# Self-attention's output projection by seven block products, and two weight loads of the first cross-attention query issued earlier

## The chip, the cores and the metric

The kernel runs on one core of one Trainium2 chip. A core has five engines that run side by side: TensorE (PE in the profile; PEld is its weight load), VectorE (DVE), ScalarE (ACT), GpSimd (POOL) and SyncE (SP), which here only issues DMA transfers. The metric is the device time of one execution in microseconds (us); less is better. Everything is in float32.

## What is computed

One decoder layer on x, 8 batches of 256 tokens with 1024 features: causal self-attention, layer norm, cross-attention to a context, layer norm, and a feed-forward part with a memory. The change touches the last product of the self-attention. In the reference that is:

```
out = jnp.einsum('bhqk,bhkd->bhqd', attn, v)
out = out.transpose(0, 2, 1, 3).reshape(bsz, q_len, HIDDEN)
return out @ wo.T
...
x = _layernorm(x + _L0_attn_ref(x, L0_attn_wq, L0_attn_wk, L0_attn_wv, L0_attn_wo), axis=-1)
```

For each batch this is a product of the heads' outputs (256 tokens x 1024) with a 1024 x 1024 matrix, added to x. The change's second part touches the query projection of the cross-attention, `q = query @ Wq`.

## The kernel before, in words

`self_attention` runs 64 steps, s = 8b + c: batch b (0 to 7), chunk c (0 to 7) of 128 features, that is four heads of 32. Even and odd steps differ: a step with odd s multiplies the weights of two chunks with the values (`weighted`, L322, in two parts) and writes the two chunks' outputs, transposed, into one tile `oT` (L347, six buffers). A step also computes scores and softmax of the next chunk (`scores`, L264), the query projection of the chunk after next (`query`, L259), one item of `others` (L406), and up to four "products" of the cross-attention's keys and values, which are computed ahead in the steps 4 to 59 (L497, L525). The last steps, 62 and 63, take the first products of the cross-attention's queries in their place.

`project_out(b, i)` (L367) is the output projection. It is an item of `others` in the steps c = 0 to 3 of the following batch, b + 1: item i computes 128 tokens x 512 columns with eight matmuls of 128x512 (two instructions each, since a float32 matmul shows as two) into one PSUM bank, and VectorE adds the bank to x, which lies in `res` (L378). Behind i = 2 and 3 it also takes the layer norm's moments (L380); GpSimd computes the reciprocal root (L132), and the normalisation itself (L383) comes in the next step. The steps c = 5 and 6 transpose the result and store it (`turn`, L389).

Its weights come through `load_out` (L359): a half of the matrix, four transfers of 512 KB, into the tile `sa_wo` with four buffers. Half 0 is issued at the end of step c = 6, half 1 at the end of step c = 1 (L571, L581).

Three engines run in the order in which the program is written: PE, POOL and SP (`manual_schedule`, L98). SP's transfers are one queue: a transfer whose buffer isn't free yet holds all behind it. Most weights pass through `weights` (L105), which hands out one of nine buffers (`w4`, W4 = 9) and issues the load at once. The order on VectorE and ScalarE is set by a planner at build time, from modelled costs.

The cross-attention's projections are already done by a seven-product scheme (`seven`, L736): for a matrix cut in 2 x 2 blocks, seven block products and some additions replace eight block products. Its weight sums are formed by GpSimd during the self-attention and stored in DRAM: `sum_event` (L489) issues the loads of one sum and finishes the one before it (four additions or subtractions, L423, and the stores). `steps` (L485, L486) says in which step which event falls: 16 events for keys and values in the steps 1 to 14, the rest from step 15 on. In `seven`, each product that needs a new weight loads it when it is called (p1, p6, p5, p4; L773, L784, L790, L807); with `eager` only p1's weight is loaded ahead (L743). `eager` is used once, for the first query: `xa_early` (L615), called at the end of step 61, calls `xa_query(0, eager=True)` and then issues the loads of x1 (the self-attention's result, transposed, L642), of the rope tables (L664) and of the first keys (L668). Those go to memory that the self-attention's own buffers held until then.

Of the kernel before, what the change touches and what calls it, by code (L numbers as in the profile page):

```python
# [71 lines left out]
class Layer:  # L72
# [74 lines left out]
    def self_attention(self):  # L147
# [78 lines left out]
            nc.vector.tensor_tensor(turned, turned, sin, ALU.mult)  # L226
            nc.vector.tensor_tensor(dst, turned, dst, ALU.add)

        kTs, vs, v_d, qTs, ats, oTs = {}, {}, {}, {}, {}, {}

        def keys(b, i):
            if i == 0:
# [89 lines left out]
        def weighted(s, rest):  # L322
# [29 lines left out]
                )  # L352
            for u in range(2):
                oTs[s - 1 + u] = oT[:, u, :]

        wos = {}
        norms = []

        def load_out(b, half):  # L359
            cols = slice(half * 512, (half + 1) * 512)  # L360
            wos[b, half] = []
            for c in range(0, KC, 2):
                w = sp.tile([P, 2, 512], F32, name="sa_wo", bufs=4)
                nc.sync.dma_start(out=w, in_=a["sa_wo"][:, c : c + 2, cols])
                wos[b, half].append(w)

        def project_out(b, i):  # L367
            half, tt = divmod(i, 2)
            t = 2 * b + tt
            cols = slice(half * 512, (half + 1) * 512)  # L370
            ps = self.mm()
            for c in range(KC):
                nc.tensor.matmul(  # L373
                    ps, lhsT=oTs[b * KC + c][:, tt * P : (tt + 1) * P], rhs=wos[b, half][c // 2][:, c % 2, :],
                    start=(c == 0), stop=(c == KC - 1),
                )
            x = self.res[t]
            nc.vector.tensor_tensor(x[:, cols], ps, x[:, cols], ALU.add)  # L378
            if half == 1:
                mv, rstd = self.moments(x, EPS)  # L380

                def norm():
                    nc.vector.tensor_scalar(x, x, mv[:, 0:1], rstd, ALU.subtract, ALU.mult)  # L383
                    self.x1[t] = self.dram.tile([P, E], F32, name=f"x1_{t}")
                    nc.scalar.dma_start(out=self.x1[t], in_=x)

                norms.append(norm)

        def turn(b, tt):  # L389

# [15 lines left out]
        def others(s):  # L406
# [1 line left out]

            b, c = divmod(s, KC)
            parts = []  # L410
            if b and c < 4:
                parts.append(lambda: project_out(b - 1, c))
            elif c < 4 or 1 < b + 1 < B:
                parts.append([
# [36 lines left out]
        def sums_of_outputs(g, u, half):  # L451
# [13 lines left out]
            def run():  # L465
# [6 lines left out]
                    nc.gpsimd.dma_start(out=self.wsums["xa_wo", g][i][:, u, cols], in_=t)  # L472
            return run


        sums = [lambda n=n, m=m, i=i: sums_of_inputs(n, m, i)
                for m in range(XA_KV // 2) for n in ("xa_wk", "xa_wv") for i in range(2)]
        sums += [lambda m=m, i=i: sums_of_inputs("xa_wq", m, i) for m in range(QP) for i in range(2)]
        sums += [lambda g=g, u=u, i=i: sums_of_outputs(g, u, i)
                 for g in range(XA_KV) for u in range(2) for i in range(2)]  # L480

        n = XA_KV * 2
        steps = [1 + e * 7 // 8 for e in range(n)]  # L485
        steps += [15 + e * (KV_END - 17) // (len(sums) - n) for e in range(len(sums) - n + 1)]  # L486
        made = []

# [26 lines left out]
        for s in range(last):  # L515
# [61 lines left out]
                event()  # L577
            if c == 7 and b + 1 < B:
                load_values(b + 1, 0)
            if b and c == 1:  # L580
                load_out(b - 1, 1)  # L581
            if b and c == 0 and b + 1 < B:
                load_x(b + 1)
            if first:
# [151 lines left out]
    def seven(self, name, m, xb, turned, done, eager=False):  # L736
# [4 lines left out]
        now = {}  # L741
        if eager:
            now["a"] = self.weights([P, KC, XA_D], self.a[name][2 * m])  # L743

        def product(w, block):
            ps = self.mm()
# [34 lines left out]
            add(now["c1"][:, :S], ps, now["p1"])  # L781

        def p6():
            now["s24"] = self.weights([P, KC, XA_D], self.wsums[name, m][0])  # L784
            ps = product(now["s24"][:, :4, :], "T2")
            now["u2"] = half()
            add(now["u2"], ps, now["p1"])

        def p5():
            now["s31"] = self.weights([P, KC, XA_D], self.wsums[name, m][1])  # L790
            ps = product(now["s31"][:, 4:, :], "T1")
            now["u5"] = half()
            add(now["u5"], ps, now["u2"])
# [811 lines left out]
```

## Time and profile before

| what | value |
|---|---|
| median of three runs | 3473.19 us (3465.23, 3473.19, 3473.85) |
| the profiled execution: its own time / its span | 3463.37 us / 3461.6 us |
| mean granted TensorE clock in it | 0.988 |
| busy share of the span: PE, PEld, DVE, ACT, POOL | 97%, 71%, 61%, 35%, 30% |
| the self-attention's share of the span | about the first 1240 us |
| `project_out`'s matmuls (L373) on the chain that ended last | 6% of the span |

The page gives for each engine the time in which it was busy, the chain of work that ended last (followed back from the last instruction, at each step to what released it), and groups of instructions: line, engine, operation, output<-inputs, shape, count, then busy time and mean duration of one, then the idle time just before them and what ended it. The windows view gives the busy time of every engine, the granted clock and the DMA engines' share for a stretch of time; the timeline lists instructions in order, with the idle time of their engine before them in brackets. Matmul instructions overlap, so a group's time on the path is read from the chain, not from the mean duration.

### The profile page before, as it was taken

Reading aid. Unit: us, or ns where it says so; the run is one execution under the profiler, and the core shown is the slowest. Engines: PE = TensorE matmul, PEld = TensorE weight load, DVE = VectorE, ACT = ScalarE, POOL = GpSimd, SP = SyncE. Lnnn points to the kernel's source line nnn. Section 1 sums busy time; section 2 is a strip of 40 time slices with the busy share of each in tenths; the row PEclk is TensorE's granted clock in tenths of the full one; section 3 lists DMA queues with packets and bytes.
Section 4 is the critical chain, followed back from the end, with each engine's and each line's share of the span. In section 5 each row is a group of like instructions: output and inputs, shape, how many; then the busy total and the mean of one; then the engine's idle time right before and its main releaser. Section 6 shows DMA issues by size and latency. Waiting matters only on the chain.

```text
span 3461.6 us, 71080 instructions
## 1 busy us (share of the span) xinstructions
PE 3369.3 (97%) x27811; PEld 2443.5 (71%) x27811; DVE 2109.8 (61%) x6003; ACT 1202.3 (35%) x4030; POOL 1044.9 (30%) x1363
## 2 busy tenths in 40 slices
PE   8999999999999799999999999999999999999996
PEld 6787778787777567777767667667667766766763
DVE  4655556565565455665685666675666666566556
ACT  3444334333443343333233332233333323333224
POOL 3444655666665121111221111112111212121112
PEclk9999999999999899999999999999999999999998
DMA  7777788787886464444544344444444544344442
GB/s 254 236 258 250 269 268 279 257 273 258 296 271 221 156 215 141 143 135 134 171 149 140 123 134 142 150 137 156 138 128 133 167 142 147 128 132 135 129 146 98
DMA packets 269710, 626.36 MB, mean 181 GB/s; under 512 B 28992, under 2 KB 99792, under 8 KB 268480
## 3 DMA queue, kind: packets, MB, share of 16 engines
q1 hardware_dynamic: 194832, 441.00, 38.9%
q0 software_dynamic: 50032, 154.66, 13.8%
q10 hardware_dynamic: 24512, 26.15, 2.2%
q8 instruction: 221, 3.62, 0.4%
q14 instruction: 113, 0.93, 0.1%
HBM read 526.93 MB, written 94.77 MB: 180 GB/s over the span
## 4 chain that ended last, share of the span: by engine, by line
PE 87%; DVE 6%; DMA 2%; ACT 2%; POOL 2%; issue 2%; SPq 0%; POOLq 0%; DVEq 0%; ACTq 0%
PE mm L757 26%; PE mm L963 20%; PE mm L214 7%; PE mm L910 7%; PE mm L373 6%; PE sc L859 6%; PE mm L751 5%; PE sc L339 3%; PE mm L1241 2%; PE mm L243 1%; PE sc L273 1%; PE mm L1018 1%; POOL acc L992 1%; ACT att L295 1%; DMA w<-in_sa_wq 0%
## 5 line engine op out<-in xcount | busy, mean ns | idle before, releaser
L757 PE MATMUL mm<-x1T,w 128*128 128x256 f32 x3584 | 851.9, 382 | 13.7 <-DMA w<-xa_wq_sums 10.8
L757 PEld LDWEIGHTS mm<-x1T,w 128*128 128x128 f32 x3584 | 676.9, 190 | 199.0 <-issue 94.8
L963 PE MATMUL mm<-w,xoS 128*128 128x512 f32 x992 | 449.2, 595 | 0.0
L873 ACT ACTIVATE xatt<-xatt,nmax 128x256 f32<-128x256 f32 x512 | 257.2, 503 | 508.1 <-DVE nmax L868 496.2
L676 POOL DMA_DIRECT2D v<-v x256 | 150.9, 596 | 735.1 <-PE mm L910 617.1
L963 PE MATMUL mm<-w,xoT 128*128 128x512 f32 x744 | 338.1, 596 | 5.3 <-ACT xoT L918 4.1
L963 PEld LDWEIGHTS mm<-w,xoS 128*128 128x128 f32 x992 | 184.9, 190 | 193.1 <-issue 170.9
L214 PE MATMUL mm<-xT,w 128*128 128x256 f32 x1280 | 305.0, 395 | 3.1 <-DMA xT<-in_xT 2.9
L763 DVE TENSOR_TENSOR half<-mm,half 128x256 f32<-128x256 f32 x288 | 119.7, 416 | 291.1 <-PE mm L757 273.2
L214 PEld LDWEIGHTS mm<-xT,w 128*128 128x128 f32 x1280 | 245.4, 196 | 54.8 <-issue 19.0
L910 PEld LDWEIGHTS mm<-xat,v 32*128 32x128 f32 x8192 | 244.3, 187 | 53.4 <-issue 29.3
L929 POOL TENSOR_TENSOR xoS<-xoT 128x512 f32<-128x512 f32 x62 | 79.0, 1274 | 671.8 <-ACT xoT L918 671.5
L910 PE MATMUL mm<-xat,v 32*128 32x128 f32 x8192 | 270.2, 278 | 5.4 <-DVE acc L970 4.4
L295 ACT ACTIVATE att<-att,nmax 128x128 f32<-128x128 f32 (+1 forms) x512 | 225.5, 442 | 143.0 <-DVE nmax L290 142.8
L859 PE MATMUL sc<-kT,qT 128*128 128x256 f32 x1024 | 262.7, 380 | 0.0
L879 ACT ACTIVATE xatt<-xatt,rec 128x256 f32<-128x256 f32 x512 | 231.1, 499 | 88.0 <-DVE rec L877 87.6
L918 ACT COPY xoT<-mm 128x128 f32<-128x128 f32 x512 | 98.0, 276 | 470.2 <-PE mm L910 439.2
L763 DVE TENSOR_TENSOR raw<-mm,half 128x256 f32<-128x256 f32 x384 | 159.1, 414 | 159.3 <-PE mm L757 118.3
L423 POOL TENSOR_TENSOR ws<-ws 128x256 f32<-128x256 f32 x320 | 242.1, 757 | 26.2 <-DMA ws<-in_xa_wk 5.7
L963 PEld LDWEIGHTS mm<-w,xoT 128*128 128x128 f32 x744 | 138.7, 190 | 148.1 <-issue 127.3
L893 DVE STREAM_TRANSPOSE xat<-xatt 128x512 f32<-128x512 f32 x256 | 180.8, 707 | 74.6 <-ACT xatt L879 71.9
L373 PE MATMUL mm<-sa_wo,sa_oT 128*128 128x512 f32 x512 | 224.8, 592 | 0.0
(230 smaller groups left out, 4859.9 us busy)
## 6 DMA issues: line engine op xcount, KB each, us to landing
w<-xa_wq_sums SPq DMA_DIRECT2D x128, 512.0 KB, 3.6
w<-xa_wo_sums SPq DMA_DIRECT2D x124, 512.0 KB, 3.6
w<-in_xa_wo SPq DMA_DIRECT2D x97, 512.0 KB, 4.2
w<-in_sa_wq SPq DMA_DIRECT2D x64, 512.0 KB, 9.1
sa_wo<-in_sa_wo SPq DMA_DIRECT2D x64, 512.0 KB, 7.0
w<-in_xa_wq SPq DMA_DIRECT2D x64, 512.0 KB, 3.5
v<-v POOLq DMA_DIRECT2D x256, 128.0 KB, 3.1
w<-xa_wk_sums SPq DMA_DIRECT2D x32, 512.0 KB, 8.5
```

What stands on the lines that cost most here:

```text
L214: nc.tensor.matmul(ps[:, :S], lhsT=lhs[:, k, :], rhs=xT[:, k, :], start=(k == 0), stop=(k == KC - 1),)
L295: nc.scalar.activation(att[:, jj, lo:hi], att[:, jj, lo:hi], AF.Exp, bias=nmax[:, i : i + 1], scale=-1.0, accum_out=sums[:, i : i + 1],)
L373: nc.tensor.matmul(ps, lhsT=oTs[b * KC + c][:, tt * P : (tt + 1) * P], rhs=wos[b, half][c // 2][:, c % 2, :], start=(c == 0), stop=(c == K ...
L423: nc.gpsimd.tensor_tensor(out, in0, in1, op)
L757: nc.tensor.matmul(ps[:, :S], lhsT=w[:, k, :], rhs=rhs[:, k, :], start=(k == 0), stop=(k == 3))
L763: nc.vector.tensor_tensor(out, in0, in1, ALU.add)
L859: nc.tensor.matmul(sc[:, qt, :], lhsT=qT[:, q0 : q0 + P], rhs=kT[:, b * S : (b + 1) * S], start=True, stop=True,)
L873: nc.scalar.activation(att[:, qt, :], att[:, qt, :], AF.Exp, bias=nmax[:, qt : qt + 1], scale=-1.0, accum_out=sums[:, qt : qt + 1],)
L879: nc.scalar.activation(att[:, qt, :], att[:, qt, :], AF.Identity, bias=0.0, scale=rec[:, qt : qt + 1])
L893: self.nc.vector.transpose(self.ats[M, b][:, :, u].rearrange("p c t j -> p t c j"), self.atts[H][b].rearrange("p t (c j) -> p t c j", j=32),)
L910: nc.tensor.matmul(banks[i][:, :P], lhsT=v[rows, c, :], rhs=at[rows, c, :], start=(c == 0), stop=(c == BLOCKS - 1),)
L963: nc.tensor.matmul(ps, lhsT=oT[lhs][:, u, off + p * P : off + (p + 1) * P], rhs=w[:, u, :], start=(u == 0), stop=(u == 1),)
```

## The change

For the batches b = 1 to 6 the four items of `project_out` are replaced by `out_by_seven(b, c)`. The heads' outputs are cut into blocks A11, A12 (tokens 0 to 127; features 0 to 511 and 512 to 1023), A21, A22 (tokens 128 to 255), the matrix into B11 to B22 of 512 x 512. Seven products of four matmuls (128x512) each, P1 to P7, use A11, A12, A22 and four sums of blocks S1 to S4 on the one side, and B11, B21, B22 and four sums T1 to T4 on the other. Each product goes into one PSUM bank, and VectorE adds it to one to four quarters of x. Batches 0 and 7 keep `project_out`.

- S1 to S4 are formed by VectorE from the `oT` tiles (`sum_heads`, two instructions of 128x256 each): S1 and S2 at the end of step c = 7, S4 and S3 at the end of the next batch's step c = 1, in two new buffers `sa_S`.
- T1 to T4 are formed once by GpSimd (`sums_of_sa`, eight events put between those of keys and values) and stored in DRAM (`sa_sums`). The first 16 events become 24 in the steps 1 to 15.
- The weights still go through the four buffers `sa_wo`, which hold two products' weights. They are now loaded at four places: P1, P2 at the end of c = 6; P6, P5 at the end of c = 0; P3, P4 at the end of c = 1; P7 at the end of c = 2. That is 14 transfers of 512 KB for a batch, before 8.
- The first cross-attention query's loads of its two summed weights (`s24`, `s31`) move from p6 and p5 (step 62) to the call in `xa_early` (step 61), ahead of the loads of x1, the tables and the keys.

```
+        PARTS = {
+            "P1": ("A11", (0, 0)), "P2": ("A12", (1, 0)), "P3": ("S4", (1, 1)), "P4": ("A22", "T4"),
+            "P5": ("S1", "T1"), "P6": ("S2", "T2"), "P7": ("S3", "T3"),
+        }
+        def load_seven(b, names):
...
+                for c in range(0, 4, 2):
+                    w = sp.tile([P, 2, 512], F32, name="sa_wo", bufs=4)
+                    if isinstance(src, str):
+                        nc.sync.dma_start(out=w, in_=sa_sums[int(src[1]) - 1][:, c : c + 2, :])
...
+        def sum_heads(b, name):
+            out = sp.tile([P, 4, P], F32, name="sa_S", bufs=2)
...
+            op, x, y = {
+                "S1": (ALU.add, heads(b, 1, 0), heads(b, 1, 1)),
+                "S2": (ALU.subtract, sevens.get((b, "S1")), heads(b, 0, 0)),
+                "S4": (ALU.subtract, heads(b, 0, 1), sevens.get((b, "S2"))),
+                "S3": (ALU.subtract, heads(b, 0, 0), heads(b, 1, 0)),
+            }[name]
+            for o, u, v in zip(pieces, x, y):
+                nc.vector.tensor_tensor(o, u, v, op)
...
+        def seventh(b, n):
...
+            for k in range(4):
+                nc.tensor.matmul(
+                    ps, lhsT=left[k // 2][:, k % 2, :], rhs=w[k // 2][:, k % 2, :],
+                    start=(k == 0), stop=(k == 3),
+                )
...
+        def out_by_seven(b, c):
+            if c == 0:
+                add_to(b, seventh(b, "P1"), (0, 0), (0, 1), (1, 0), (1, 1))
+                add_to(b, seventh(b, "P2"), (0, 0))
+            elif c == 1:
+                add_to(b, seventh(b, "P6"), (0, 1), (1, 0), (1, 1))
+                add_to(b, seventh(b, "P5"), (0, 1), (1, 1))
+            elif c == 2:
+                add_to(b, seventh(b, "P3"), (0, 1))
+                norm_later(2 * b)
+                add_to(b, seventh(b, "P4"), (1, 0))
+            else:
+                add_to(b, seventh(b, "P7"), (1, 0), (1, 1))
+                norm_later(2 * b + 1)
...
+        for e in range(8):
+            sums.insert(3 * e + 2, lambda e=e: sums_of_sa(e // 2, e % 2))
...
-        n = XA_KV * 2
-        steps = [1 + e * 7 // 8 for e in range(n)]
+        n = XA_KV * 2 + 8
+        steps = [1 + (e - e // 3) * 7 // 8 for e in range(n)]
...
+            if c == 7 and 0 < b < B - 1:
+                sum_heads(b, "S1")
+                sum_heads(b, "S2")
+            if c == 0 and 0 < b - 1 < B - 1:
+                load_seven(b - 1, ("P6", "P5"))
+            if c == 2 and 0 < b - 1 < B - 1:
+                load_seven(b - 1, ("P7",))
             if b and c == 1:
                 load_out(b - 1, 1)
+                if 0 < b - 1 < B - 1:
+                    load_seven(b - 1, ("P3", "P4"))
+                    sum_heads(b - 1, "S4")
+                    sum_heads(b - 1, "S3")
...
         if eager:
             now["a"] = self.weights([P, KC, XA_D], self.a[name][2 * m])
+            for i, sums in enumerate(("s24", "s31")):
+                now[sums] = self.weights([P, KC, XA_D], self.wsums[name, m][i])
```

(`add_to` issues one VectorE addition of 128x512 for each pair it is given; `norm_later` is the moments and the normalisation as before; `load_out(b, 0)` calls `load_seven(b, ("P1", "P2"))` for these batches.)

## The prediction

> **What bounds the kernel now.** I read the page's busy shares first, then windows of the self-attention, then the chain, the waits and the timelines around one batch and around the hand-over to the cross-attention.
>
> ```profile
> span 3461.6 us, 71080 instructions
> ...
> PE 3369.3 (97%) x27811; PEld 2443.5 (71%) x27811; DVE 2109.8 (61%) x6003; ACT 1202.3 (35%) x4030; POOL 1044.9 (30%) x1363
> ```
>
> The same shares hold inside the stage that changes. Two of its windows (columns: width, then busy us of PE, PEld, DVE, ACT, POOL, then granted clock, DMA share, GB/s):
>
> ```profile
> 300.00:400.00 100.00, 95.27 (x985) 72.18 (x984) 54.36 (x187) 34.70 (x130) 59.33 (x74) 0.97 0.69 234
> ...
> 600.00:700.00 100.00, 100.00 (x1002) 74.70 (x1001) 62.28 (x224) 41.89 (x158) 61.07 (x78) 1.00 0.76 268
> ```
>
> Inside a batch PE never rests; where it does (4.7 us in the first window), the timeline shows the start of a context quarter. So a PE instruction taken out in the middle of a batch should shorten the span by its own time, as long as nothing else is late. The timeline of PE shows the four items that change (batch 3, computed in batch 4's steps 0 to 3) and, later, the hand-over:
>
> ```profile
> 607.11 7.03 PE L373 MATMUL mm<-sa_wo,sa_oT 128*128 128x512 f32 x16
> ...
> 626.90 7.03 PE L373 MATMUL mm<-sa_wo,sa_oT 128*128 128x512 f32 x16
> ...
> 649.61 7.03 PE L373 MATMUL mm<-sa_wo,sa_oT 128*128 128x512 f32 x16
> ...
> 666.90 7.03 PE L373 MATMUL mm<-sa_wo,sa_oT 128*128 128x512 f32 x16
> ```
>
> ```profile
> 1165.35 4.45 PE L757 MATMUL mm<-x1T,w 128*128 128x256 f32 x16
> 1180.56 14.00 PE L757 MATMUL mm<-x1T,w 128*128 128x256 f32 x56 [10.75 <-DMA w<-xa_wq_sums]
> ```
>
> The bracket is the largest single wait of PE in the stage: the first query's p1 and p2 are done at 1169.8, and p6 waits 10.75 us for a summed weight. SP's timeline says why:
>
> ```profile
> 1104.52 0.33 SPq L109 DMA_DIRECT2D w<-in_xa_wq  x1
> 1156.04 2.03 SPq L642 DMA_DIRECT2D x1T<-x1T  x4
> ...
> 1169.38 1.92 SPq L364 DMA_DIRECT2D sa_wo<-in_sa_wo  x4
> 1171.34 1.20 SPq L109 DMA_DIRECT2D w<-xa_wq_sums  x2
> 1172.58 1.21 SPq L109 DMA_DIRECT2D w<-in_xa_wq  x2
> ```
>
> SP reached the eager load at 1104.5, was held until 1156.0 (x1T goes into memory that the last query projection frees) and again until 1169.4 ahead of `sa_wo`; the sums were behind both.
>
> **Part 1, matmuls.** A batch had 4 items x 16 instructions; it gets 7 products x 8 = 56, eight fewer. On the chain an item of 16 takes 6.87 us, 0.429 us each. 8 x 0.429 = 3.44 us a batch, six batches: **-20.6 us**, all on the path by the windows.
>
> **Part 1, VectorE.** The rows nearest to what is added (columns: count, then busy, mean ns, idle before and its releaser):
>
> ```profile
> L378 DVE TENSOR_TENSOR res<-mm,res 128x512 f32<-128x512 f32 x29 | 19.9, 686 | 88.8 <-PE mm L373 83.8 <-DMA xa_wq_sums<-ws 5.0
> ...
> L227 DVE TENSOR_TENSOR sa_qT<-mm,sa_qT 128x256 f32<-128x256 f32 x64 | 26.7, 418 | 1.8
> ```
>
> Additions from PSUM go from 4 to 14 a batch: 10 x 0.686 = 6.9 us. The block sums are 8 x 0.418 = 3.3 us. Together 10.2 us a batch, 61 us in all, on an engine that is idle for about 38 us of every 100. Is it hidden where it falls? P1's four additions come at 610.6, when the planner has the softmax's transposes up to 613.4; `weighted` needs them at 621.9, a cover of 8.5 us against 2.7. P6's three (630.4) fall in VectorE's idle 629.0 to 634.0. P5's second addition and S4, S3 (0.7 + 1.7 = 2.4 us) come at 634 to 640, ahead of the row maxima that free the score banks: they end at 642.03 and PE wants the bank at 645.19, a cover of 3.2 us. S1 and S2 (1.7 us) meet the same point at 750.7 against 753.8. So the cover holds, by 0.8 us at the tightest place. It is missing where a context quarter starts inside these steps (two of the three): there PE already waits (3.1 us at 333.7, for the maxima), so the 2.4 us can show. Bounds 0 to 5 us, I take +1.5. All of it exposed would be +61, none is the lower end; nothing in it can gain.
>
> The strided sums have two SBUF inputs, which no row shows in that form. The nearest is the rope's product L732: median 0.687, mean 0.857, one at 2.106, so an excess of 0.17 each: 48 x 0.17 = 8 us of VectorE time, under the same cover. The Trainium skill ("SBUF — State Buffer", section "SBUF: two separate sides") speaks against the change here: a VectorE instruction with two SBUF inputs and a GpSimd instruction exclude each other for their whole length. By it each of the 48 sums could be held for one GpSimd addition; the row's mean says most are not.
>
> **Part 1, GpSimd.** Eight more sum events. The page's events follow each other by 8.9 us when back to back (81.83 to 90.75): the four operations, and the waits of their two buffers.
>
> ```profile
> L423 POOL TENSOR_TENSOR ws<-ws 128x256 f32<-128x256 f32 x320 | 242.1, 757 | 26.2 <-DMA ws<-in_xa_wk 5.7
> ```
>
> 8 x 8.9 = 71 us in the first 300, in which POOL has 170 us idle. Step 8 gets three events (27 us in a step of 16), so POOL lags by up to 9 us through the steps 9 to 15. What waits for POOL there is the layer norm's root: VectorE has waited for it 12 times, at most 5.0 us; two such waits fall in steps 10 and 11. Bounds 0 to 10 us, I take +2. T1 to T4 are complete in step 15, by this lag at about 298 us, an estimate from the same 8.9 us, and loaded from then on: the first P6 (item 1 at 313.85) has 16 us, two landings.
>
> **Part 1, SP and DMA.** The four buffers make P6/P5, P3/P4 and P7 wait for the products before them, so SP stands still at three places a batch instead of one:
>
> ```profile
> SPq L364 <- PE mm L373: 190.7, 32, 29.2
> ...
> sa_wo<-in_sa_wo SPq DMA_DIRECT2D x60, 512.0 KB, 7.2
> ```
>
> The one that exists (628.8 to 634.3) costs PE nothing: the weights queued behind it (634.4 on) come in time. The items of steps 0 to 2 keep 16 instructions, so the places in time stay as shown: P1's first buffer is free a quarter of an item after 607.1, at 608.8, and P6 comes at 626.9, 18 us for a landing of 7.2 (longest 13.2). P3 has 628.6 to 649.6, 21 us; P7 has 651.3 to 666.9, 16 us. Behind SP in step 0 are the next x (needed in step 4) and step 1's weights (used 20 us later). The 3 MB more a batch meet a DMA share of 0.42 to 0.74 in 607 to 627, but 1.02 in 627 to 634. I take 0; bounds 0 to 3 us for each of the 18 new waits, 54.
>
> **Part 2, the query's loads.** They need two of nine w4 buffers at SP's position of 1104.5; the last key/value products (to 1138) free more than that, so they land 30 us before use. They delay nothing: x1T behind them is held until 1156 anyway. Then p6, p5, p3, p7 run from 1169.8 (their blocks T2, T1, T3 are made by 1170.4): 4/7 of 14.0 = 8.0 us, to 1177.8. **Next late** is p4's own weight, still behind `sa_wo`: it is issued at 1171.3, and loads issued there landed after 9 to 10 us: 1181. Three products of 1.93 us follow, to 1186.8, where before ended 1194.55: 7.8. I take **-7**; bounds 0 (if all of it becomes the next wait) and -12.4 (the whole 10.75, and the 1.7 us that the clock of 0.62 cost from 1180.5 to 1185).
>
> The clock's rows: 1.00 up to 1146, 0.54 to 0.78 from the softmax wait at 1146 to 1185. The Trainium skill ("TensorE: Matmul & The Clock Gate", section "What's actually happening") has half clock after an idle window of about 3.4 us. By it the four products would take 4 x 8 x 0.456 = 14.6 us (twice the 3.65 us / 16 of a full-speed item of L214), to 1184.4, and the gain would be 4; the trace's 1165 to 1169 ran at 0.76 with the same history.
>
> **Sum.** -20.6 - 7 + 1.5 + 2 = **-24.1 us**. Against the profiled execution: 3463.37 (span 3461.6 and 1.8 around it) gives 3439.3. The median lies 9.8 above that execution; from it, 3473.19 - 24.1 = **3449**.
>
> **Rivals.**
> - *The query part moves its wait to p4 entirely.* For: p4's weight stays behind `sa_wo`. Against: four products fit ahead of it. -20.6 + 3.5: 3456.
> - *VectorE shows.* A quarter of its 61 us is exposed at the score banks. For: covers of 3.2 and 3.1 us against 2.4 and 1.7. Against: 5 us idle stretches each step. -24.1 + 15: 3464.
> - *The stage is paced by the softmax chain, not PE.* Then eight matmuls less a batch only widen PE's waits, and -7 is left: 3466. For: PE's waits that exist are for maxima and transposes. Against: windows at 100.00.
> - *Slower: `sa_wo` comes late.* The weights of the product pair in steps 1, 2 and 3 land after PE wants them, 3 us each: 18 x 3 = 54, -24.1 + 54 = +30: 3503. For: DMA share over 1.0 in places, twice as many 512 KB loads in three steps. Against: landings of 7.2. It decides from landings of 17 us on: the 16 to 21 us above, and then 24.1 / 18 = 1.3 us for each wait.
>
> **How the numbers follow.** Forecast 0.64 (its own range 3438 to 3458), query part lost 0.08, VectorE 0.15, softmax pace 0.05, `sa_wo` late 0.08. About 0.3%, 10.4 us, is what a measurement can tell from no change: faster means below 3462.8. Faster: 0.64 + 0.08 + half of 0.15 = 0.79; same: the other half and 0.05 = 0.13; slower 0.08. The range goes from the profiled execution's base less 32 us (20.6 and nearly all of the 12.4) to the softmax case: 3431 to 3466; the late `sa_wo` is left out.
>
> **What would show it.** Right: 48 fewer 128x512 matmuls at 0.429 us; a batch shorter by 3.4 us; windows still at 100; PE's wait for `xa_wq_sums` at the hand-over gone, one of some 3 us for `in_xa_wq` in its place. Wrong: PE waits for `sa_wo`; more PE waits for maxima (L290) or transposes (L306) in steps 0 to 2; VectorE waits for the root in steps 10 and 11 of over 5 us; a late T1 to T4 at 300 us. A planner that orders VectorE otherwise than by readiness would break the covers.

## The result, and the profile after

The changed kernel is slower. Median of five runs 3487.72 us (3482.14 to 3488.16), of the kernel before in the same comparison 3465.94 us (3463.98 to 3473.85): ratio 1.0053, 95% interval 1.0041 to 1.0065. The forecast was 3449 us, so it misses by 39 us and in sign: the change was to take 24.1 us away and added 22. (The base of the forecast, a median of three, was 7 us above the median of five here.) The profiled execution took 3484.05 us, with a span of 3482.3 us and a mean granted clock of 0.984.

The page of the changed kernel: span, busy shares, and the chain of work that ended last.

```profile
span 3482.3 us, 71242 instructions
...
PE 3362.0 (97%) x27763; PEld 2440.9 (70%) x27763; DVE 2159.8 (62%) x6111; ACT 1202.3 (35%) x4030; POOL 1097.3 (32%) x1443
...
PE 68%; DMA 11%; POOL 10%; DVE 6%; issue 4%; ACT 1%; SPq 0%; POOLq 0%; DVEq 0%; ACTq 0%
PE mm L881 22%; PE mm L1089 19%; PE mm L1036 7%; PE sc L985 6%; DMA xa_wq_sums<-ws 5%; POOL ws L509 5%; PE mm L214 3%; PE mm L1367 2%; PE mm L434 2%; PE mm L875 2%; POOL ws L521 1%; DMA xa_wo_sums<-ws 1%; DMA w<-xa_wk_sums 1%; DMA sa_wo_sums<-ws 1%; PE sc L339 1%
```

The 48 instructions are gone (27811 to 27763) and PE is 7 us less busy, but the span is 20.7 us longer. The chain says who took over: before, PE held 87% of it and POOL and DMA 2% each. Now it runs, from 60 to 229 us and again from 308 to about 700, mostly along GpSimd's sum events (L509) and their stores (`sa_wo_sums<-ws`, `xa_wq_sums<-ws`). The same two windows as before the change (width, busy us of PE, PEld, DVE, ACT, POOL, clock, DMA share, GB/s):

```profile
300.00:400.00 100.00, 84.22 (x815) 60.79 (x814) 58.50 (x186) 29.32 (x110) 60.21 (x75) 0.91 0.78 269
...
600.00:700.00 100.00, 91.92 (x960) 68.48 (x959) 58.03 (x189) 29.34 (x110) 59.20 (x74) 0.95 0.88 298
```

PE is 11 and 8 us less busy in them (95.27 and 100.00 before), and the clock has dropped with it. Four of the new products in PE's timeline of the changed kernel (batch 3: P1 and P2 in one row, then P3, then P4):

```profile
624.57 7.03 PE L434 MATMUL mm<-sa_wo,sa_oT 128*128 128x512 f32 x16
...
678.10 3.60 PE L434 MATMUL mm<-sa_wo,sa_S 128*128 128x512 f32 x8
681.53 3.60 PE L434 MATMUL mm<-sa_wo,sa_oT 128*128 128x512 f32 x8
```

A product of eight takes 3.43 us on PE, half an item, as reckoned. The hand-over to the cross-attention looks as forecast, too:

```profile
1193.88 9.06 PE L881 MATMUL mm<-x1T,w 128*128 128x256 f32 x40 [1.02 <-DMA x1T<-x1T]
1207.14 8.15 PE L881 MATMUL mm<-x1T,w 128*128 128x256 f32 x24 [4.20 <-DMA w<-in_xa_wq]
```

The wait of 10.75 us for `xa_wq_sums` is gone, and one of 4.20 for p4's own weight has come in its place.

What is new is GpSimd's state. Its waits in the changed kernel (line, releaser, us in total, times, longest):

```profile
POOL ws L547 <- DMA xa_wo_sums<-ws: 105.0, 25, 7.1
POOL ws L521 <- DMA xa_wq_sums<-ws: 102.4, 22, 7.6
```

Before, these two stood at 82.5 (21 times) and 61.2 (17 times). Two buffers `ws` serve all sums, so the load of an event waits for the store of the event two before it, which was issued a moment ago. It works in order, so whatever stands behind such a load is late as well. The prediction had named a place where this would show: the layer norm's root, which GpSimd computes, in the steps 10 and 11. In the kernel before VectorE waited 0.35 and 0.68 us for the two roots of these steps. First the second of them, then the changed kernel (here and below the lines are from different engines' timelines):

```profile
214.63 0.81 DVE L383 TENSOR_SCALAR res<-res,ln_mv,ln_rstd 128x1024 f32<-128x1024 f32 x1 [0.68 <-POOL ln_rstd L132]
```

```profile
212.41 0.81 DVE L467 TENSOR_SCALAR res<-res,ln_mv,ln_rstd 128x1024 f32<-128x1024 f32 x1 [9.87 <-POOL ln_rstd L132]
...
227.66 0.81 DVE L467 TENSOR_SCALAR res<-res,ln_mv,ln_rstd 128x1024 f32<-128x1024 f32 x1 [8.19 <-POOL ln_rstd L132]
...
219.16 1.49 POOL L521 DMA_DIRECT2D ws<-in_xa_wv  x2 [6.79 <-DMA sa_wo_sums<-ws]
...
229.36 1.99 PE L273 MATMUL sc<-sa_kT,sa_qT 32*128 32x128 f32 x16 [6.81 <-ACT sa_oT L349]
```

GpSimd's load at 219.16 waits for the store of a new sum, the root of step 11 (226.83) stands behind it, VectorE waits for the root, and PE loses 6.81 us behind VectorE and ScalarE. A further 3.46 us go at 186.88, where PE waits for a summed weight (`xa_wv_sums`) that GpSimd's events have to deliver.

The second place is the start of a context quarter. (The cross-attention's keys and values are computed for a quarter of the context after another. Each quarter begins with loads of its context on SP's queue, and on GpSimd's with gathers of position tables and two block sums.) GpSimd's queue around the first such start:

```profile
335.45 1.44 POOL L521 DMA_DIRECT2D ws<-in_xa_wq  x2 [6.12 <-DMA xa_wq_sums<-ws]
...
348.80 1.44 POOL L521 DMA_DIRECT2D ws<-in_xa_wq  x2 [6.83 <-DMA xa_wq_sums<-ws]
...
362.22 1.42 POOL L521 DMA_DIRECT2D ws<-in_xa_wq  x2 [2.51 <-DMA xa_wq_sums<-ws]
...
368.84 1.03 POOL L805 DMA_INDIRECT w<-in_xa_table,pos_u  x1 [0.30 <-PE mm L434]
...
378.28 0.58 POOL L132 TENSOR_TENSOR ln_rstd<-ln_ve,neghalf 128x1 f32<-128x1 f32 x1
```

Events come 13.4 us apart, most of it store time, and behind them stand the gathers of the position tables (345.96 before) and, behind the gathers and two block sums of the context, the layer norm's root (355.42 before). VectorE stands for that root, and PE behind VectorE. VectorE also waits longer for the quarter's context; there, first the kernel before, then the changed one:

```profile
331.30 1.23 DVE L646 TENSOR_TENSOR ctxT<-ctxT 128x1024 f32<-128x1024 f32 x1 [4.88 <-DMA ctxT<-in_ctxT]
333.69 0.51 PE L273 MATMUL sc<-sa_kT,sa_qT 32*128 32x128 f32 x4 [3.10 <-DVE nmax L290]
```

```profile
351.09 1.78 DVE L768 TENSOR_TENSOR ctxT<-ctxT 128x1024 f32<-128x1024 f32 x1 [9.95 <-DMA ctxT<-in_ctxT]
354.04 0.80 PE L273 MATMUL sc<-sa_kT,sa_qT 32*128 32x128 f32 x4 [8.72 <-DVE nmax L290]
...
378.89 0.81 DVE L467 TENSOR_SCALAR res<-res,ln_mv,ln_rstd 128x1024 f32<-128x1024 f32 x1 [10.18 <-POOL ln_rstd L132]
```

The maxima (`nmax`), for which PE waits, stand directly behind the context's addition on VectorE in every one of the twenty traces, so the planner's order does not differ between the kernels at this place. Behind the late root PE waits another 6.58 us, until 380.36, for an addition (L443) that is queued behind this L467. At the second quarter's start PE waits 5.95 us (644.45) for a gather; before, it waited for none there. In all VectorE waits 38.6 us for roots at L467, before 12.5 (at L383).

**How the runs are compared.** Besides medians (each beside runs of the kernel before on the same chip) the text uses one table worked out from the traces: when PE starts the first score matmul (L273) of step s, less the same in the kernel before, and how much this delay grows from step 8 to 16, 16 to 24 and so on. A context quarter starts in the steps 18, 32 and 46. Up to step 8 the delay is left out: it lies between -4 and +6 us even in kernels that issue the same there.

| kernel | 8-16 | 16-24 | 24-32 | 32-40 | 40-48 | 48-56 | 56-63 | sum |
|---|---|---|---|---|---|---|---|---|
| after | 12.5 | 8.0 | -4.8 | 7.6 | 2.0 | -0.8 | -1.9 | 22.6 |
| e3, query only | 0.0 | -0.8 | 0.6 | 1.1 | 0.9 | 2.1 | 1.4 | 5.4 |
| e2, sums only | 12.6 | 6.6 | -0.2 | 1.1 | 2.5 | 0.1 | 0.4 | 23.2 |
| e8, sums, 3 buffers | 1.5 | 3.7 | -0.5 | 0.6 | 2.9 | 0.2 | 0.6 | 9.1 |
| e1, no sums | 0.0 | 4.7 | -3.9 | 5.2 | -0.1 | -2.2 | -2.4 | 1.4 |
| e5, e1 with 8 loads | 0.0 | -0.9 | -3.9 | 2.3 | -1.9 | -3.5 | -3.0 | -10.9 |
| e6, e1 with a light VectorE | 0.0 | 2.0 | -3.8 | 3.4 | 1.4 | 0.4 | -2.4 | 1.1 |
| e7, both | 0.0 | -1.5 | -1.0 | 0.2 | -0.7 | -3.5 | -2.7 | -9.1 |
| e9, after, 3 buffers | 0.0 | 10.3 | -3.5 | 5.4 | -0.1 | 0.0 | -2.6 | 9.5 |
| e11, e7, 3 buffers | 4.2 | -0.9 | -1.0 | 1.2 | -1.6 | -3.5 | -2.3 | -3.8 |
| e12, e6, 3 buffers | 0.9 | 2.8 | -1.8 | 1.1 | -0.5 | 4.7 | -1.9 | 5.2 |
| e13, e7, events earlier | 0.0 | 8.6 | -0.1 | 10.7 | 11.7 | -3.5 | -1.7 | 25.7 |
| e14, three batches | 0.3 | 2.6 | 20.1 | 8.3 | 12.4 | 13.5 | -3.0 | 54.2 |
| e15, e14, 3 buffers, events earlier | 1.4 | 15.1 | 2.7 | 17.0 | 5.9 | 0.2 | -2.1 | 40.2 |
| e16, no products, earlier | 1.5 | 7.0 | -0.2 | 8.0 | 4.8 | 0.2 | 1.0 | 22.4 |
| e17, e9, events later | 1.5 | 3.9 | 0.6 | -3.9 | -7.0 | 0.5 | -2.4 | -6.9 |
| e18, no products, later | 2.0 | -1.8 | -1.9 | 0.4 | -3.3 | 0.5 | 1.3 | -2.8 |

Each row is one execution. Row e3 shows the scatter: up to step 61 it issues what the kernel before issues, and it still reads 5.4 in sum. So sums are read to about 5 us, single stretches to 2.

### The profile page after: what moved, and what is told of

Its sections match the earlier page's. It is cut to its first block, busy times and chain, and to the rows that moved or that the text cites. A ratio compares the mean times of both kernels' runs of the same rounds, so it can differ in the third digit from the quotient of the medians.

```text
span 3482.3 us, 71242 instructions
## 1 busy us (share of the span) xinstructions
PE 3362.0 (97%) x27763; PEld 2440.9 (70%) x27763; DVE 2159.8 (62%) x6111; ACT 1202.3 (35%) x4030; POOL 1097.3 (32%) x1443
## 4 chain that ended last, share of the span: by engine, by line
PE 68%; DMA 11%; POOL 10%; DVE 6%; issue 4%; ACT 1%; SPq 0%; POOLq 0%; DVEq 0%; ACTq 0%
PE mm L881 22%; PE mm L1089 19%; PE mm L1036 7%; PE sc L985 6%; DMA xa_wq_sums<-ws 5%; POOL ws L509 5%; PE mm L214 3%; PE mm L1367 2%; PE mm L434 2%; PE mm L875 2%; POOL ws L521 1%; DMA xa_wo_sums<-ws 1%; DMA w<-xa_wk_sums 1%; DMA sa_wo_sums<-ws 1%; PE sc L339 1%
## 5 line engine op out<-in xcount | busy, mean ns | idle before, releaser
L214 PE MATMUL mm<-xT,w 128*128 128x256 f32 x1280 | 307.1, 397 | 3.3 <-DMA xT<-in_xT 3.3
L214 PEld LDWEIGHTS mm<-xT,w 128*128 128x128 f32 x1280 | 247.2, 197 | 55.5 <-issue 20.6
L509 POOL TENSOR_TENSOR ws<-ws 128x256 f32<-128x256 f32 x352 | 265.6, 755 | 28.0 <-DMA ws<-in_xa_wk 5.5
L881 PE MATMUL mm<-ctxT,w 128*128 128x256 f32 x896 | 213.3, 390 | 18.7 <-DMA w<-xa_wk_sums 8.0
```

What stands on the lines that cost most here:

```text
L214: nc.tensor.matmul(ps[:, :S], lhsT=lhs[:, k, :], rhs=xT[:, k, :], start=(k == 0), stop=(k == KC - 1),)
L509: nc.gpsimd.tensor_tensor(out, in0, in1, op)
L881: nc.tensor.matmul(ps[:, :S], lhsT=w[:, k, :], rhs=rhs[:, k, :], start=(k == 0), stop=(k == 3))
```

## The experiments

**Four parts, one at a time (e1 to e4).** The first theory: GpSimd's eight events put its queue behind for the whole stage, and they are all of the loss. The rivals: VectorE's added work, or the `sa_wo` loads.

e1 loads columns of `sa_wo` in place of T1 to T4 and forms no sums:

```
-                        nc.sync.dma_start(out=w, in_=sa_sums[int(src[1]) - 1][:, c : c + 2, :])
+                        nc.sync.dma_start(out=w, in_=a["sa_wo"][:, c : c + 2, 0:512])
-        for e in range(8):
-            sums.insert(3 * e + 2, lambda e=e: sums_of_sa(e // 2, e % 2))
```

> The changed kernel without GpSimd's eight sum events: the four summed quarters of sa_wo are not formed, the products that would read them read columns of sa_wo itself (as many bytes, so the output differs), and the other sum events go back to the steps they had before. All else of the change stays: 56 products a batch, 14 additions, the block sums on VectorE, 14 loads of 512 KB, the query's early loads. Theory (GpSimd's queue runs late for the whole stage because of the eight events): the delays against the kernel before vanish, and the saved matmuls and the query part show: about -24 us against before, 3435 to 3447. Rival (VectorE's added work or the sa_wo loads cost the time): nothing of it is taken away, so the time stays within 6 us of the changed kernel, 3480 to 3490.

e2 adds `sums_of_sa`, the loop that puts its eight events among the others, and the changed list `steps` to the kernel before; the sums are stored and never read.

> The kernel before with the eight sum events of sa_wo on GpSimd and the changed list of steps, and nothing else: the sums are stored and never read, all products are the old ones. Theory: the whole loss is here, about +40 us against before (the changed kernel's +21 and the 20.6 of matmuls, less the query part that is not in it, so +35 to +48), 3500 to 3515. Rival (VectorE or sa_wo): within 5 us of before.

e3 puts only the hunk of `seven` (`eager`) into the kernel before.

> The kernel before with only the query's part of the change: its two summed weights are loaded ahead of x1T. Both theories: -7 us (bounds -3 to -12), about 3459, with a wait of PE for p4's own weight of 3 to 4 us in place of the 10.75 for the summed weight.

e4 stores one tile for an event:

```
-                for i, t in enumerate((b11, b22, b12, b21)):
-                    nc.gpsimd.dma_start(out=sa_sums[i][:, k, cols], in_=t)
+                nc.gpsimd.dma_start(out=sa_sums[0][:, :, k, cols], in_=w.rearrange("p i j c -> p (i j) c"))
```

> The changed kernel with one store of 512 KB for each sum event of sa_wo, into one tile in DRAM with the sums side by side, where it had four of 128 KB into four tiles. Theory with the store as the price of an event: the event gets several us shorter (three issues fewer, one landing), GpSimd's lag shrinks, and a third or more of the loss goes: 3465 to 3478. Theory with the operations as the price: under 4 us gained, 3483 to 3489. Rival (VectorE or sa_wo): no change.

Measured, beside 3468.15 us of the kernel before: e1 3459.55 (ratio 0.9978, 0.9968 to 0.9988), e2 3488.45 (1.0062, 1.0042 to 1.0082), e3 3462.62 (0.9981, 0.9971 to 0.9990), e4 3475.50 (1.0024, 1.0012 to 1.0035).

The sums alone cost 20 us (e2), and without them the change is 8.6 us faster (e1): the events are the largest part, and the loss of the changed kernel up to step 16 is theirs to the microsecond (12.6 and 12.5). But the theory wanted 35 to 48 from e2 and -24 from e1. Of e1's gain 5.5 us is the query's part (e3), so 48 matmuls bring 3 us and not 20.6. Some 17 us are lost elsewhere. e4's time fits "a third or more of the loss goes", but its rows do not show why: steps 8 to 16 lose 14.5 us as before, and the one store lands after 7.4 us where the small ones took 6.0.

**The other half: loads or VectorE (e5 to e7).** All three start from e1. e5 lets P3, P4 and P7 use weights that are already loaded, eight loads a batch:

```
+            if "P6" in names:
+                for n, other in (("P3", "P6"), ("P4", "P5"), ("P7", "P5")):
+                    sevens[b, n] = sevens[b, other]
```

> The kernel of the first experiment (no sums of sa_wo on GpSimd) with eight loads of 512 KB a batch in place of 14, as many as before: P3 takes the weights of P6, P4 and P7 those of P5 (so the output differs). Against before, the first experiment had -8.6 us and a good 17 still missing. Theory A (the extra loads make the stores and loads of GpSimd's sums land later, xa_wq_sums 5.7 us against 4.2, and GpSimd falls an event behind: late context tables at batch 4's start): 7 to 10 us come back, 3447 to 3453, and those stores land in 4.2 to 4.6 us. Theory B (VectorE's added work alone): no more than 3 us come back, 3456 to 3462.

e6 adds each product to one block and forms no S:

```
-                add_to(b, seventh(b, "P1"), (0, 0), (0, 1), (1, 0), (1, 1))
+                add_to(b, seventh(b, "P1"), (0, 0))
...
-                sum_heads(b, "S1")
-                sum_heads(b, "S2")
```

> The kernel of the first experiment with VectorE's added work cut: seven additions a batch in place of 14 (each product is added to one block only) and no block sums of the heads (the products read heads alone), so the output differs; 14 loads a batch stay. Theory A (loads): under 4 us come back, 3455 to 3460. Theory B (VectorE at the starts of the context quarters, where PE waited 7.9 us for the maxima and 2.9 for an addition at 339 to 363 in the first experiment): 6 to 10 us come back, 3449 to 3454.

e7 has both edits.

> The two cuts of the two experiments above together: eight loads a batch, seven additions, no block sums, no sums of sa_wo (the output differs). What is left of the change is eight matmuls fewer a batch and the query's early loads. If PE sets the pace and the two theories name all that is missing: -20.6 and -5.5, so -26 against before, 3439 to 3445. If the stage is paced by something else: -12 or less, over 3453.

Beside 3474.19: e5 3454.72 (0.9939, 0.9922 to 0.9956), e6 3461.81 (0.9966, 0.9955 to 0.9978), e7 3456.96 (0.9954, 0.9937 to 0.9970). In the table the six loads cost 12 us with VectorE's full work (1.4 against -10.9) and 10 without it (1.1 against -9.1); VectorE's work costs nothing to be seen (0.3, and -1.8). By the ratios the loads cost some 13 and 4 us, VectorE's work 4 and -5. B falls. A stands by e1 against e5, and later by e12 against e11 (12 us by the ratios); the pair e6 and e7 alone would not tell 4 us from none. PE never waits for `sa_wo`; the loads delay others. The landing times up to 1150 us (KB, median us from issue to landing), first of the kernel before, then of e1:

```profile
xa_wq_sums<-ws POOLq DMA_DIRECT2D x64, 256.0 KB, 4.2
```

```profile
xa_wq_sums<-ws POOLq DMA_DIRECT2D x64, 256.0 KB, 5.7
```

GpSimd waits for just these stores: 100.8 us in e1 against 61.2 before, and its gathers ahead of step 32 come at 619.96 in place of 612.49. With eight loads (e7) these stores land in 4.4 us. The gathers land later too (5.4 us in e1 for 3.3 before), but that is not the loads' doing: in e7 they take 6.0. The Trainium skill ("DMA: Bandwidth & Descriptors", section "Anatomy of one DMA — SWDGE (gpsimd) path") prices a transfer from GpSimd's queue at 2.0 us and its bytes at 436 GB/s. That makes an estimate of 2.6 us for 256 KB; the 4.2 and 5.7 measured beside other traffic are what counts here.

There is a second path, on SP's own queue. At the first quarter's start e1 has:

```profile
336.70 1.23 DVE L766 TENSOR_TENSOR ctxT<-ctxT 128x1024 f32<-128x1024 f32 x1 [9.66 <-DMA ctxT<-in_ctxT]
```

With 14 loads and a light VectorE (e6) this wait for the context is 7.23 us; with eight loads it is 0.29 (e5) and none (e7). The place counts here, not the number alone: in e1, e6 and the changed kernel four loads of `sa_wo` are issued at the end of step c = 1, just ahead of the context's, and in e5 and e7 none. The kernel before has four there as well, and waits 4.88. So at this place e5 and e7 seem relieved of something that the kernel before also pays. (These are single traces; with three buffers, below, the wait reads 4.53 to 12.43 with four loads ahead in e9, e10 and e12, and 2.52 with none in e11.)

With all of this gone, e7 gains 9 of the 20.6 us that its matmuls save. The batches whose output falls in the steps 48 to 51 and 56 to 59 show their 3.4 us; the others give it back beside the quarters' starts (batch 4's gain, in the steps 40 to 43, at step 46). There e7 still has:

```profile
361.86 3.63 PE L874 MATMUL mm<-ctxT,w 128*128 128x256 f32 x8 [8.84 <-DVE res L447]
```

VectorE's addition stood behind a layer norm that waited 10.92 us for its root on GpSimd.

**Three buffers for GpSimd's sums (e8 to e12).** If the wait for the store is the price of an event, a third buffer removes it. In e8 (on e2) and e9 to e12: `name="ws", bufs=2` becomes 3 in all sum functions. In e9 and e10 (and in e15 and e17 below) the room comes from `t2` (one buffer for two) and `half` (three for four).

> The kernel before with the eight sum events of sa_wo on GpSimd (stored, never read), as in the second experiment, and three buffers for GpSimd's sums in place of two. With two, the load of each event waits for the store issued just before it; with three for the one before that. If this wait is what an event costs (7 waits, 40 us for the stores of sa_wo_sums in the changed kernel), most of the 20 us of the second experiment goes: 3462 to 3474, and GpSimd's waits for the stores fall by more than half. If the issues and operations themselves cost it: at most 5 us go, 3482 to 3488.

> The changed kernel, whole, with three buffers for GpSimd's sums in place of two; the room comes from the rope's scratch tile (one buffer for two) and the half blocks of the key/value products (three for four). Theory (GpSimd, in order, waits at each event's load for the store issued just before, is late for the layer norm's root, the context's block sums and the table gathers, and VectorE and PE wait behind it): the 14 us lost up to batch 1's end fall to about 2 (5.5 against 13 in the kernel with the sums alone), those at the starts of the quarters by half or more: 15 to 28 us under the changed kernel, -8 to +4 against before. Rival (the lag is the events' own work, 64 us of operations and issues for eight, and the loads of sa_wo): under 6 us gained.

> The kernel above with one store of 512 KB for each sum event of sa_wo in place of four. With two buffers one store gained 12 us. If that gain was the store's landing that the next load waited for, three buffers have taken it already: within 4 us of the kernel above. If it was the three issues saved (0.7 us each, eight events, 17 us in all): 4 to 10 us under the kernel above.

> The seventh experiment (eight loads, seven additions, no block sums, no sums of sa_wo; the output differs) with three buffers for GpSimd's sums. There 11.5 of the 20.6 us of matmuls were still missing, 8.8 of them in one wait of PE behind VectorE's wait for the layer norm's root on GpSimd (360 us). Theory: that wait goes, and -24 to -28 against before shows. Rival (VectorE or PSUM paces it): no more than 3 us under the seventh experiment, -16 to -20.

> The sixth experiment (14 loads of 512 KB, seven additions, no block sums, no sums of sa_wo; the output differs) with three buffers for GpSimd's sums. If the extra loads cost time only because they make the stores that GpSimd waits for land later: the same as the run above within 3 us, -23 to -28 against before. If they also delay what SP loads (context, tables, weights): 5 to 12 us slower than the run above.

e8: 3479.74 beside 3474.19 (1.0017, 1.0007 to 1.0026), so some 15 of the sums' 20 us are gone; steps 8 to 16 lose 1.5 us in place of 12.6, and GpSimd's waits for stores are down to 0.8 us. e9: 3467.26 beside 3468.21 (0.9998, 0.9987 to 1.0008): the whole change, 19 us faster than it was by the ratios, level with before. Its stretch 16 to 24 still loses 10.3: VectorE waits 12.43 us for the first quarter's context there, and PE 10.38 behind it. e10: 3467.25 (0.9997, 0.9984 to 1.0009); with the wait gone, the issues saved are worth nothing. e11 and e12 speak against the theory: 3453.72 (0.9954, 0.9940 to 0.9968) is e7's ratio again, though the theory wanted the 11 us, and e12, at 3466.63 (0.9990, 0.9980 to 1.0000), is slower than e6. But e12 against e11 is a clean pair on the loads: the six of them cost 12 us by the ratios (9 in the table) where GpSimd has its third buffer, so they cost time by more than the stores that it waits for. Where GpSimd is not behind by eight events, a third buffer buys nothing. Of PE's 8.84 us, 4.46 remain in e11. Why e12 is slower than e6 is not settled; in its trace PE waits 6.20 and 4.65 us for `xa_wk_sums` around 883 and 953, in e6 2.09 there.

**The order at the quarters' starts (e13 to e18).** Left was the place in GpSimd's queue.

```
+        steps = [s - 1 if s in (18, 32, 46) else s for s in steps]
```

is e13's edit (on e7) and also in e15 and e16. e14 and e15 use seven products in batches 2, 4 and 6 alone (`0 < b < B - 1` becomes `b in (2, 4, 6)`, likewise for `b - 1`), with the eight events behind those of keys and values. e15 and e16 have three buffers; e16 is e3 with them, without products.

> The seventh experiment (eight loads, seven additions, no block sums, no sums of sa_wo; the output differs) with the sum events of steps 18, 32 and 46, in which a context quarter starts, moved one step forward, so that GpSimd comes to the table gathers, the context's block sums and the layer norm's root without one (6 us) ahead of them. If that event makes PE wait at the starts of the quarters: 5 to 9 of the missing 11 us come back, 3 us or less at each start, -21 to -26 against before. If the context's loads do it: within 3 us of the seventh experiment, -14 to -19.

> The changed kernel with seven products only in batches 2, 4 and 6 (of 0 to 7), whose output falls beside no start of a quarter; the others keep their four items of 16. The eight sum events of sa_wo come after those of the keys' and values' weights, in steps 15 to 20, no more than before in steps 1 to 14. Theory: no loss in the first 15 steps, 3.4 us gained in each of three batches, 5.5 for the query, and some 3 to 6 lost to GpSimd's lag at step 18: -9 to -14 against before, 3454 to 3460. If the sum events cost 20 us wherever they stand: +4 to +8.

> The kernel above with three buffers for GpSimd's sums (room from the rope's scratch tile and one half block) and no sum events in steps 18, 32 and 46. Theory: -12 to -18 against before, 3450 to 3456.

> The kernel before with the query's early loads, three buffers for GpSimd's sums and no sum events in steps 18, 32 and 46, without any product of seven. -5 to -9 against before. The difference to the kernel above is what three batches of seven products are worth with their sums: theory -6 to -10; if it is nothing, the seven products give back what they save even there.

All four went far the other way, beside 3472.11: e13 3482.90 (1.0023, 1.0014 to 1.0033), e14 3510.89 (1.0110, 1.0093 to 1.0127), e15 3503.21 (1.0085, 1.0068 to 1.0102), e16 3487.89 (1.0048, 1.0031 to 1.0066). The edit had the order reversed: `xa_context`, with the gathers, is called at the end of the steps 17, 31 and 45, so the events of the next step came ahead of it, not behind. In e13 the first quarter's gathers start at 358.16 (e7: 350.33), the root at 367.60, and VectorE:

```profile
368.22 0.81 DVE L471 TENSOR_SCALAR res<-res,ln_mv,ln_rstd 128x1024 f32<-128x1024 f32 x1 [18.50 <-POOL ln_rstd L132]
```

PE waits 16.4 us there, and over all quarters 20.6 us for gathers (e7: 2.2). Three events moved by one step cost 24 us by the ratios, and 35 us of self-attention between the two traces (-9.1 to 25.7), with not one instruction more. e14 shows the other limit of the same engine. It has no such move, but 72 events in the steps 15 to 57 in place of 64: 1.67 a step. In its trace events follow each other by 12.4 us on average (steps 18 to 58), which makes 20.7 us at 1.67 a step; the steps there take 20.6 us, in the kernel before 18.6 (285.9 to 1160.9 us over 47 steps). So the pace of the events fits that of the steps. VectorE waits 73.0 us for roots, 15 times, and batches without a quarter beside them lose, too. With three buffers (e15) the stretches 24 to 32 and 48 to 56 lose 2.7 and 0.2 us in place of 20.1 and 13.5; the rest of e15's loss stands at the quarters' starts, where it has the reversed order.

e17 (on e9) and e18 (e16 without the wrong line) move the events behind the gathers:

```
+        steps = [s + 1 if s in (17, 31, 45) else s for s in steps]
```

> The ninth experiment (the whole change with three buffers for GpSimd's sums) with the sum events of steps 17, 31 and 45 moved to the steps 18, 32 and 46, behind the table gathers, the context's block sums and the layer norm's root of a quarter's start. Theory (GpSimd's order at the quarters' starts holds the rest of the loss, some 25 us of it in the ninth experiment): the gathers come 6 us earlier and 8 to 16 us come back: 3452 to 3460, -0.25 to -0.5% against before. If the context's loads or the sa_wo loads hold it: within 4 us of before.

> The kernel before with the query's early loads, three buffers for GpSimd's sums and the events of steps 17, 31 and 45 moved one step back, without any product of seven. The loss at the quarters' starts is small in before (PE waits of 3.1, 0.9 and 2.9 us), so -6 to -10 against before. If it is as fast as the kernel above, the seven products are worth nothing even with GpSimd out of the way; theory: the kernel above is 2 to 8 us faster.

Beside 3468.77: e17 3452.81 us (0.9959, 0.9945 to 0.9973), e18 3455.07 (0.9956, 0.9943 to 0.9970). e17 is the whole change, by the ratios 14 us faster than before and 33 faster than the changed kernel. Its queue at the first quarter, the gathers and the root:

```profile
343.72 1.04 POOL L806 DMA_INDIRECT w<-in_xa_table,pos_u  x1 [0.31 <-DMA w<-xa_wk_sums]
...
353.20 0.58 POOL L132 TENSOR_TENSOR ln_rstd<-ln_ve,neghalf 128x1 f32<-128x1 f32 x1
```

VectorE's longest wait for a root is 1.4 us, and PE's wait for the addition at that place, 4.21 us in e9, is gone. VectorE's wait for the context reads 3.47 us for e9's 12.43, and PE's behind it 1.39 for 10.38. How much of that is the order's doing stays open, since e10, which has e9's order, reads 6.37. e16 and e18 differ in the line of the events alone, without any product: 32 us by the ratios, 25 in the table. But e18, without a single product of seven, is as fast within the intervals. What makes the two fast is GpSimd's order, the third buffer and the query's loads. The products themselves, with their sums and loads, are worth 4 us in the table (-6.9 against -2.8), which is inside the scatter. Three batches give their 3.4 us (steps 32 to 48 and 56 to 63); in steps 16 to 32 and 48 to 56 it goes again, with PE waits of 3.76 us (326.86, ended by nothing that the profile shows), 3.29 (394.44, for `sa_qT`) and 1.67 (920.62, for an addition), none of them for `sa_wo`. That the extra loads are behind these is likely from e5, but no run took them out of e17: that stays open.

## Why the prediction was wrong

- **The bound.** "A PE instruction taken out in the middle of a batch should shorten the span by its own time" held: where no quarter is near, a batch gains 3.4 us. That nothing else is late did not hold at the quarters' starts. The prediction read the 4.7 us of idle PE in the window 300 to 400 as a small exception, with VectorE's own work as the only thing that could add to it. It was the sign that PE is paced by other queues there: 3.10 us of it stood behind VectorE's wait for the context on SP's queue (331.30), and in the changed kernel that wait and GpSimd's late root made 15 us of it.
- **Matmuls, -20.6.** In size right, 0.429 us each. With all other parts of the change taken away, 9 us reached the end of self-attention (e7, read to about 5); a batch's 3.4 us are there in its own steps and are given back at the next quarter's start.
- **VectorE, +1.5, bounds 0 to 5.** About right: nothing that the runs can show, 0.3 and -1.8 us in the table. The additions took 0.677 us (0.686 reckoned), the block sums 0.48 to 0.53 (0.418 and an excess of 0.17). The exclusion of GpSimd that the Trainium skill gives ("SBUF — State Buffer", section "SBUF: two separate sides") could hold a sum for as long as a GpSimd addition, 0.755. The groups' means are at most 0.11 above the 0.418 and their medians 0.416 to 0.426, so most sums were not held; single ones took up to 0.99.
- **GpSimd, +2, bounds 0 to 10: the step that failed.** In the prediction's words: "8 x 8.9 = 71 us in the first 300, in which POOL has 170 us idle", "POOL lags by up to 9 us through the steps 9 to 15". The runs showed 20 us (e2), and 21 in the table (after against e1): 12.5 up to step 16, the rest from the first quarter's start on, where the gathers and roots stand in the same queue. The sign that the prediction had set itself, waits of over 5 us for the roots in the steps 10 and 11, came: 9.87 and 8.19. Two errors are in the sum. The 8.9 us came from two events at 81 to 91 us; in the changed kernel events follow each other by 11.2 us on average from 64 to 301 us, where the eight were put, and by 13.4 at 335 to 362, because a load waits for the last store. At this distance 24 events make 270 of the first 300 us, an estimate from the 11.2: the queue has hardly room left, and its lag is not one of up to 9 us that begins with step 8. And GpSimd's idle time was counted as room for any order, though it is time spent waiting for others in a queue that then runs in order. The waits to be read were GpSimd's for its own stores, 61 and 82 us in the trace of before, all of them behind 300 us, where its events stand closer (12.6 us apart on average for 15.5).
- **SP and DMA, 0, bounds 0 to 54.** Right that `sa_wo` is never late: PE has no wait for it. Wrong that more traffic then costs nothing: 9 to 12 us in the table (4 to 13 by the ratios). Two paths are seen, stores that GpSimd waits for and the context behind `sa_wo` on SP's queue; how the cost divides between them, and over other paths, stays open. Neither the forecast nor the rival "`sa_wo` comes late" had either.
- **Query, -7.** -5.5 (e3: -3.5 to -10 by the interval), with the forecast wait for p4's weight, 4.20 us for some 3. The prediction's slower estimate, 0.456 us a matmul at half clock, did not show: in the changed kernel 40 of them took 9.06 us from 1193.88 on, 0.227 each.
- **The sum.** In place of -20.6 + 1.5 + 2 + 0 the table has -9 + 0 + 21 + 10 = 22 for self-attention, where 22.6 was measured. That this closes proves nothing, since the terms are differences of the same rows (e7; e1 less e6; after less e1; e6 less e7); what supports it is that the sums alone, added to the kernel before, read 23.2 (e2), or 18 less e3's 5.4. No rival named GpSimd; the slow one was given the right sign for the wrong wait.

## What to carry to other kernels

An engine that works in order and stands 40% idle is not free for more: look at what its waits are for, and at what stands behind the place where the new work goes. Price an added load-compute-store event by the distance of two events where it will stand, with the store's landing in it when buffers are few. Before saving matmuls, see which stretches run at less than 100% of PE, and what each wait in them ends on: time saved beside them comes back only when their own pace is mended, and here mending that (with the query's loads), without the new products, was worth as much.

## What the hardware showed that was not expected

- Eight small sums (256 KB loads, four operations, stores) cost 20 us on a queue that was idle for much of the time. A third buffer took some 15 of them back.
- Order alone, with the same instructions, is worth 24 us of 3460 by the ratios (35 between two traces): three events one step earlier (e13 against e7). Between e16 and e18 it is 32.
- Behind short waits the granted clock was lower. In e1 PE waits 1.24, 0.68 and 0.57 us within 627 to 630, and the next 5 us ran at a granted clock of 0.66: 16 matmuls of L214 take 4.67 us in place of 3.72. Whether just these waits did it no run shows.
- With 3 MB more a batch from SP's queue 256 KB stores from GpSimd's queue landed after 5.7 us (e1) in place of 4.4 (e7) and 4.2 (before).
